# Keeping the FFN's hidden values in PSUM pairs through the FP4 quantizer, in a planned kernel

## The chip, the cores and the metric

The kernel runs on one core of a Trainium2 chip. A core has a matrix engine (PE, whose weight loads are shown apart as PEld), a vector engine (DVE), a scalar engine (ACT), GpSimd (POOL), a queue that issues transfers (SP) and sixteen DMA engines. On-chip memory is SBUF, and PSUM with eight banks of 512 float32 values in each of 128 partitions; PE writes its products to PSUM. The metric is the device time of one execution in microseconds, the median of several runs.

## The reference

The input x has shape (4, 2048, 256). Four residual layers follow each other, each on the layer-normed x: attention A, an FFN, attention B, and the same FFN once more.

```python
def fp4_quant_dequant(x):          # blocks of 16 along the last dim
    xb = x.reshape(shape[:-1] + (shape[-1] // BLOCK, BLOCK))
    scale = jnp.max(jnp.abs(xb), axis=-1, keepdims=True) / 6.0
    scale = jnp.maximum(scale, jnp.float32(1e-12))
    xn = xb / scale
    idx = jnp.searchsorted(_MID, jnp.abs(xn))
    q = _GRID[idx] * jnp.sign(xn) * scale
...
    gate = fp4_linear(x, w_gate)   # 256 -> 704
    y = fp4_linear(x, w_up)        # 256 -> 704
    h = jax.nn.silu(gate) * y
    return fp4_linear(h, w_down)   # 704 -> 256
...
    x = x + _L0_attn_a_ref(_layernorm(x), ...)
    x = x + _L0_ffn_ref(_layernorm(x), ...)
    x = x + _L0_attn_b_ref(_layernorm(x), ...)
    x = x + _L0_ffn_ref(_layernorm(x), ...)
```

`fp4_linear` quantizes both its input and its weight. Attention B mixes the four samples that share a position (its first axis); attention A needs two norms over the whole tensor, which a first pass over x supplies.

## The kernel before

**Tiles.** There are 16 groups j of 128 positions, each with four samples s, so a group is a tile of [128, 4, 256]. In each group the two FFNs (k = 1 and 2) handle one sample at a time: 16 x 2 x 4 = 128 FFN tiles of [128 rows, 704 hidden values].

**The plan.** Nothing is issued in the order of the source. `plan.op(engine, us, rank, fn, reads, writes, ...)` records an operation with its engine, a cost in microseconds and a due time; tokens of the form (buffer, part) give the dependences. `Plan.order` then lists the operations by a simple simulation of the engines: of the operations that are ready on an engine, the one due first is taken, provided that its buffers are free. A buffer is taken from its pool by the first operation that names it and goes back after the last one. `LATE` and `SYNC` are delays between an operation and one that depends on it on another engine; on the same engine the delay is 0. An operation with `port=True` keeps such operations of DVE and POOL apart in the plan. `BEGIN` holds six offsets for each group, the due times of its stages. Each engine then executes its list in order and waits at semaphores.

**PSUM.** Eight banks in two pools of four: `mm` for the hidden products and the first pass's weight products, `bank` for all else (transposes, projections, the down product).

**An FFN tile** (`ffn_tile`, L1436) goes through these steps:

1. PE, L1447: for each half of 352 columns, the gate product into one `mm` bank and the up product into another; two chunks of 128 along the contraction, and two records in the trace for each float32 matmul.
2. ACT, L1468: silu of the gate bank into the SBUF tile `sil`.
3. DVE, L1479: `sil` times the up bank into the SBUF tile `h` (pool of 3). `h` has 17 columns for each block of 16; the seventeenth holds 6e-12, the floor of the block's largest value.
4. `to_grid` (L1209): DVE takes each block's largest absolute value with the padding column (L387) and its reciprocal (L388), both in one planned operation; DVE multiplies `h` by -6 times the reciprocal into `qa` (L392); ACT writes |qa| x 2^22 as bfloat16 into `qm` (L398), whose rounding is the grid's; DVE takes max(qm, floor) + qa in place (L405) and max(qm, floor) - qa into `qm` (L408). These three DVE passes are marked `port=True`.
5. `scales_turned` (L1278): PE transposes the tile's 44 scales (L1286), ACT copies them (L1294), SP spreads them over `hqT` by six transfers (L1303).
6. SP transposes `qm` into `gT` by a DMA (L1505); POOL multiplies `hqT` by `gT` (L1514).
7. PE makes the down product from `hqT` (L1551); DVE adds it to x (L339, or L1583 in the second FFN, after which SP stores x, L1591).

The last group's second FFN multiplies the scales in before the transpose and transposes on PE (L1527), with `qa` kept.

**Around it.** The FFN's input is quantized likewise in tiles of 1024 (`xn`, `qax`, `qmx`). `turn` (L1146) transposes a group with PE and ACT; `project` (L1175) makes attention's products; L1329 drains a 512-wide product with a per-row factor; L1784 adds halves of attention B's weighted values in SBUF; L718 floors the scales of the weights; L1053 and L1080 belong to the weights' preparation, which runs once.

Of the kernel before, what the change touches and what calls it, by code (L numbers as in the profile page):

```python
# [12 lines left out]
BF16 = mybir.dt.bfloat16  # L13
# [5 lines left out]
P = 128  # L19
D = 256  # L20
# [4 lines left out]
HF = FF // 2  # L25
FB = FF // BLK

# [30 lines left out]
class Plan:  # L58
# [4 lines left out]
    SYNC = {"POOL": 0.12}  # L63
    LATE = {"PE": 0.163, "DVE": 0.08, "ACT": 0.097, "POOL": 0.04}
# [50 lines left out]
    def order(self, seed):  # L115
# [58 lines left out]
        while left:  # L174
# [58 lines left out]
            while done and done[0][0] <= now + 1e-9:  # L233
# [8 lines left out]
                for n in ops[i]["then"]:  # L242
                    ops[n]["left"] -= 1
                    f = ops[n]["engine"]
                    late = 0.0 if f == e else self.LATE.get(e, 0.0) + self.SYNC.get(f, 0.035)
# [8 lines left out]
def kernel(  # L254
# [43 lines left out]
    banks = [one([P, 512], f"bank{i}", ps) for i in range(8)]  # L298
# [86 lines left out]
    def to_scales(src, amax, rs):  # L385

        nc.vector.tensor_reduce(amax, src, AX.X, ALU.max, apply_absolute_value=True)  # L387
        nc.vector.reciprocal(rs, amax)  # L388

# [30 lines left out]
    plan.pool("mm", banks[:4])  # L420
    plan.pool("bank", banks[4:])
# [4 lines left out]
    floored += tiles("h", 3, [P, FB, BLK + 1], fp)  # L426
# [3 lines left out]
    tiles("sil", 2, [P, HF], fp)  # L430
    tiles("qa", 3, [P, FF], fp)

    for t in tiles("qm", 2, [P, 6 * P], fp, BF16):
        nc.gpsimd.memset(t[:, FF:], 0.0)
    tiles("gT", 2, [P, 6, P], fp, BF16)
# [3 lines left out]
    for t in tiles("hqT", 3, [P, 6, P], fp):  # L439
        nc.gpsimd.memset(t[P // 2 :, 5, :], 0.0)  # L440
# [15 lines left out]
    def first_pass():  # L456
        op = plan.op
        GRAM = [plan.given("bank", 2) for _ in range(KC)]
        gram = [b.ap for b in GRAM]

# [194 lines left out]
        for ns in together:  # L655
# [39 lines left out]
            if n >= SOON:  # L695
                op("POOL", 4.635, at + 3.0, lambda cut=cut: roots_later(cut), seen, done)
            else:
                y, _, v = (norm_tiles["a"][:, cut, i, :] for i in range(2, 5))
                op("DVE", 0.592, at + 0.5, lambda cut=cut: variances(cut), seen, done)
                op(  # L700
                    "ACT",
                    0.194,
# [6 lines left out]
                op("DVE", 0.962, at - 30.0, lambda cut=cut: inverses(cut), (), done)  # L709
# [119 lines left out]
        for i in range(2):  # L829
# [7 lines left out]
            for h in range(2):  # L837
# [10 lines left out]
                op("PE", 0.328, at + 8, turn, [(a, 0)], [(tp, 0)])  # L848
# [24 lines left out]
            0.622,  # L873
# [14 lines left out]
            0.407,  # L888
# [6 lines left out]
        def fold(at, dst, token, lhs):  # L895

            mm = plan.buf("mm")

            def pe():
# [19 lines left out]
                0.372,  # L919
# [6 lines left out]
        def center(at, w, n, tokens, bias=None):  # L926
# [3 lines left out]
            mm = plan.buf("mm")  # L930
# [48 lines left out]
        def times_biases():  # L979
# [15 lines left out]
            2.828,  # L995
# [14 lines left out]
        def take_sums():  # L1010
# [3 lines left out]

        op("DVE", 0.28, FIRST, take_g00, [(b, 0) for b in GRAM], [(G, 0)])
        op("DVE", 0.474, FIRST, take_rest, [(b, 0) for b in GRAM], [(G, 1)])
        op(
            "DVE", 0.847, FIRST + 1.0, take_sums, [(b, 0) for b in GRAM] + [("cross", 0)], [("part", 1)]
        )
        for c in range(KC):  # L1020
            mm = plan.buf("mm")
# [10 lines left out]
            def square(c=c, mm=mm):  # L1032
# [13 lines left out]
                "DVE", 0.714, FIRST, square, [(mm, 0), (WQK, 0)], [(PROD, c), ("part", 2 + c)]  # L1046
            )

        tot = plan.buf("mm")

        def total():
# [9 lines left out]
            0.187,  # L1061
# [8 lines left out]
            0.172,  # L1070
# [16 lines left out]
        def join_biases():  # L1087
# [7 lines left out]
        op("DVE", 2.447, FIRST, join_weights, [(MK, "m")], [("rn", 0), ("wvz z", 0)])  # L1095
        op(
            "DVE",
            1.501,
# [12 lines left out]
        (-456, -237, -412, -522, 134, -290),  # L1111
        (-168, -284, -45, 104, -606, 332),
        (119, 225, 211, 262, 362, 408),
        (143, 422, 246, 352, 80, 421),
        (147, 285, 233, 408, -700, 482),
        (388, -717, 369, 471, 380, 544),
        (460, -155, 484, 464, 544, 653),
        (536, -344, 284, 622, 569, 721),
        (545, 595, 595, 701, 520, 834),
        (563, 82, 635, -690, 342, 187),  # L1120
        (626, 675, 709, 812, 126, 892),
        (600, 340, 689, 490, 597, 906),
        (647, 956, 776, 896, 236, 1043),
        (705, 1053, 316, 796, 610, 936),
        (889, -178, 774, 528, -698, 1416),
        (873, 1096, 427, 1046, 274, 496),
    ]

    def group(j):

        begin = BEGIN[j][0]
        X = kept[j] if j in kept else plan.buf("x")
# [753 lines left out]
```

## Time and profile before

| | |
|---|---|
| Time, median of 3 runs | 1492.98 us (1492.23 to 1496.39) |
| The profiled execution | 1495.64 us |
| Its span, first to last instruction | 1493.9 us |
| Instructions in the span | 19989 |
| Mean granted PE clock | 0.999 |
| DMA | 220990 packets, 96.87 MB |
| HBM | 18.09 MB read, 8.39 MB written |
| First hidden product | 114.6 us after the span's start |
| Last hidden product ends | some 1472.1 us |

The page gives busy time for each engine and then in 40 slices of the span, where a digit is a tenth of busy time. Groups of instructions are shown with their line, engine, operation, output and input tiles, shapes and count; behind the bar come the idle time before them and what ended it. "Mean" durations include the part of an instruction that overlaps the next one's start. The views by source line add the least, the median and the largest duration. Some lines of the 40 slices:

```profile
PE   7989999999999999999999999999999999999998
DVE  6899999999899899999999999999898999999985
ACT  6556646543745463666565465453357443555332
POOL 5344656625746354653635555662747354565442
```

and of the engines' idle time, by what was waited for (total us, times, longest):

```profile
POOL hqT L1514 <- DMA gT<-qm: 128.0, 33, 11.1
ACT qm L398 <- DVE qa L392: 109.5, 64, 5.3
ACT qm L398 <- DMA gT<-qm: 26.4, 11, 5.4
PE bank L1551 <- POOL hqT L1514: 10.9, 14, 1.9
PE bank L1447 <- DVE h L1479: 4.9, 5, 1.8
```

### The profile page before, as it was taken

Reading aid. Unit: us, or ns where it says so; the run is one execution under the profiler, and the core shown is the slowest. Engines: PE = TensorE matmul, PEld = TensorE weight load, DVE = VectorE, ACT = ScalarE, POOL = GpSimd, SP = SyncE. Lnnn points to the kernel's source line nnn. Section 1 sums busy time; section 2 is a strip of 40 time slices with the busy share of each in tenths; the row PEclk is TensorE's granted clock in tenths of the full one; section 3 lists DMA queues with packets and bytes.
Section 4 is the critical chain, followed back from the end, with each engine's and each line's share of the span. In section 5 each row is a group of like instructions: output and inputs, shape, how many; then the busy total and the mean of one; then the engine's idle time right before and its main releaser. Section 6 shows DMA issues by size and latency. Waiting matters only on the chain.

```text
span 1493.9 us, 19989 instructions
## 1 busy us (share of the span) xinstructions
PE 1440.6 (96%) x5742; PEld 998.6 (67%) x5742; DVE 1373.4 (92%) x2139; ACT 793.4 (53%) x1694; POOL 767.5 (51%) x787
## 2 busy tenths in 40 slices
PE   7989999999999999999999999999999999999998
PEld 6746666667666666766666666666766656767776
DVE  6899999999899899999999999999898999999985
ACT  6556646543745463666565465453357443555332
POOL 5344656625746354653635555662747354565442
PEclk9999999999999999999999999999999999999999
DMA  8403321234432324434223322332522423423441
GB/s 255 119 0 49 53 53 28 40 61 88 70 60 54 67 54 86 84 74 62 34 48 56 68 54 50 67 55 50 103 39 41 75 48 67 66 40 72 85 85 35
DMA packets 220990, 96.87 MB, mean 65 GB/s; under 512 B 108240, under 2 KB 220624, under 8 KB 220880
## 3 DMA queue, kind: packets, MB, share of 16 engines
q1 hardware_dynamic: 220880, 95.60, 32.9%
q8 instruction: 45, 0.74, 0.2%
q14 instruction: 65, 0.53, 0.1%
HBM read 18.09 MB, written 8.39 MB: 18 GB/s over the span
## 4 chain that ended last, share of the span: by engine, by line
PE 58%; DVE 25%; issue 5%; DMA 4%; ACT 4%; POOL 4%; SPq 0%; POOLq 0%; ACTq 0%; DVEq 0%
PE bank L1447 27%; PE bank L1551 14%; PE bank L1177 12%; DVE qa L405 3%; PE bank L1154 2%; DVE qa L392 2%; DVE pp L1658 2%; DVE qm L408 2%; DVE h L1479 2%; DVE sh L387 2%; DVE sc L1665 2%; DMA gT<-qm 2%; DVE x L339 1%; POOL hqT L1514 1%; DVE vz L1329 1%
## 5 line engine op out<-in xcount | busy, mean ns | idle before, releaser
L1447 PE MATMUL bank<-wguT,turned 128*128 128x352 f32 x2048 | 637.0, 461 | 7.7 <-DVE h L1479 4.9
L1447 PEld LDWEIGHTS bank<-wguT,turned 128*128 128x128 f32 x2048 | 380.5, 190 | 213.4 <-issue 12.5
L1514 POOL TENSOR_TENSOR hqT<-hqT,gT 128x768 f32<-128x768 f32 x124 | 229.2, 1852 | 304.2 <-DMA gT<-qm 128.0
L1551 PE MATMUL bank<-wdT,hqT 128*128 128x256 f32 x1536 | 352.5, 381 | 11.6 <-POOL hqT L1514 10.9
L1551 PEld LDWEIGHTS bank<-wdT,hqT 128*128 128x128 f32 x1536 | 288.7, 190 | 73.7 <-POOL hqT L1514 21.5
L398 ACT ACTIVATE qm<-qa 128x704 bf16<-128x704 f32 (+2 forms) x136 | 105.9, 780 | 142.1 <-DVE qa L392 109.5
L1468 ACT ACTIVATE sil<-bank 128x352 f32<-128x352 f32 x256 | 114.7, 455 | 110.3 <-PE bank L1447 88.0
L405 DVE SCALAR_TENSOR_TENSOR qa<-qm,qa 128x704 f32<-128x704 bf16 (+2 forms) x136 | 147.9, 1088 | 15.1 <-ACT qm L398 14.8
L1479 DVE TENSOR_TENSOR h<-sil,bank 128x352 f32<-128x352 f32 x256 | 128.6, 509 | 29.3 <-ACT sil L1468 17.3
L1766 POOL TENSOR_TENSOR pp<-vg,sc 128x1024 f32<-128x1024 f32 x64 | 137.8, 2169 | 23.9 <-DVE tok L1787 20.9
L392 DVE SCALAR_TENSOR_TENSOR qa<-sh,h 128x704 f32<-128x704 f32 x128 | 132.2, 1040 | 1.1
L408 DVE SCALAR_TENSOR_TENSOR qm<-qm,qa 128x704 bf16<-128x704 bf16 x124 | 126.9, 1024 | 2.5
L1177 PE MATMUL bank<-wvz,turned 128*128 128x512 f32 x256 | 117.5, 596 | 8.1 <-ACT turned L1161 4.5
L387 DVE TENSOR_REDUCE sh<-h 128x44 f32<-128x748 f32 x128 | 119.1, 931 | 3.8
L1177 PE MATMUL bank<-wqkB,turned 128*128 128x512 f32 x256 | 120.5, 593 | 0.9 <-ACT qk L1646 0.9
L1270 POOL TENSOR_TENSOR qax<-qax,sx 128x1024 f32<-128x1024 f32 x32 | 70.1, 2190 | 75.1 <-DVE qax L408 65.0
L1161 ACT COPY turned<-bank 128x512 f32<-128x512 f32 x160 | 85.9, 586 | 30.5 <-PE bank L1154 30.3
L345 ACT ACTIVATE dev<-x,norms_f 128x256 f32<-128x256 f32 x128 | 64.8, 506 | 46.3 <-DVE x L339 43.8
L1177 PEld LDWEIGHTS bank<-wvz,turned 128*128 128x128 f32 x256 | 46.6, 190 | 57.4 <-issue 40.6
L1658 DVE TENSOR_TENSOR pp<-qk 128x1024 f32<-128x1024 f32 x64 | 82.0, 1281 | 1.9 <-ACT qk L1646 1.9
L381 ACT ACTIVATE xn<-x,norms_f 128x256 f32<-128x256 f32 x128 | 67.6, 591 | 21.8 <-POOL norms_f L375 16.5
L1665 DVE TENSOR_REDUCE sc<-pp 128x64 f32<-128x1024 f32 x64 | 77.8, 1215 | 1.3
(193 smaller groups left out, 2030.2 us busy)
## 6 DMA issues: line engine op xcount, KB each, us to landing
hqT<-sT SPq DMA_DIRECT2D x620, 64.0 KB
x<-in_L_attn_a_x_dram SPq DMA_DIRECT2D x23, 512.0 KB
out_dram<-x SPq DMA_DIRECT2D x64, 128.0 KB
hqT<-sT SPq DMA_DIRECT2D x124, 32.0 KB
gT<-qm SPq DMA_TRANSPOSE x124
hqT<-in_L_ffn_w_down_dram SPq DMA_DIRECT2D x2, 352.0 KB
hqT<-in_L_ffn_w_gate_dram SPq DMA_DIRECT2D x5, 128.0 KB
hqT<-in_L_ffn_w_up_dram SPq DMA_DIRECT2D x5, 128.0 KB
```

The costliest lines, as they stand in the source:

```text
L387: nc.vector.tensor_reduce(amax, src, AX.X, ALU.max, apply_absolute_value=True)
L392: nc.vector.scalar_tensor_tensor(blocks(a), over_blocks(rs), -6.0 * BELOW, src, ALU.mult, ALU.mult)
L405: nc.vector.scalar_tensor_tensor(a, m, FLOOR, a, ALU.max, ALU.add)
L408: nc.vector.scalar_tensor_tensor(a if to is None else to, m, FLOOR, a, ALU.max, ALU.subtract)
L1177: nc.tensor.matmul(bank.ap[:, :n], lhs.ap[:, c, s * P : (s + 1) * P], w[:, c, :], start=(c == 0), stop=(c == KC - 1),)
L1447: nc.tensor.matmul(bank.ap[:, :HF], xqT.ap[:, c, s * P : (s + 1) * P], w[:, c, cols], start=(c == 0), stop=(c == KC - 1),)
L1468: lambda g=g, sil=sil: nc.scalar.activation(sil.ap, g.ap[:, :HF], AF.Silu),
L1479: lambda u=u, sil=sil, half=half: nc.vector.tensor_mul(h.ap[:, half * FB // 2 : (half + 1) * FB // 2, :BLK], blocks(sil.ap), blocks(u.ap[: ...
L1514: lambda: nc.gpsimd.tensor_mul(hqT.ap, hqT.ap, gT.ap),
L1551: nc.tensor.matmul(o.ap[:, :D], hqT.ap[:, i, :], wdT[:, i, :], start=(i == 0), stop=(i == 5),)
L1658: nc.vector.tensor_mul(pr.ap, qk.ap[:, s : s + 1, :D].to_broadcast([P, S, D]), qk.ap[:, :, D:],)
L1766: nc.gpsimd.tensor_mul(pv.ap.rearrange("p t (n e) -> p t n e", e=HD), vg.ap[:, :, :D].rearrange("p t (n e) -> p t n e", e=HD), over_blocks ...
```

## The change

**PSUM and pools.** The eight banks become two pairs of two banks and four single banks; the pool `mm` and the tile `h` are gone. The gate product of the first 512 columns takes a single bank; a pair takes the up product (704 values over both banks), the gate product of the last 192 columns behind it, and, once those are used, the 44 block maxima. `qa` goes from 3 tiles to 2, `qm` from 2 to 4, `gT` from 2 to 3 and `hqT` from 3 to 4. `sil` becomes two kinds of tile, of 512 and 192.

**The FFN tile.** The hidden product is cut at 512 instead of 352. DVE multiplies `sil` into the up values in place, in PSUM. The reduction reads PSUM without a padding column and writes the maxima to PSUM; a new DVE operation applies the floor into `sh`; the reciprocal is an operation by itself. The passes run in place in PSUM and the last one writes `qm` (or `qa`) in SBUF. They are no longer marked `port=True`.

**The plan.** `SAME` adds a delay between dependent operations of one engine; many costs are smaller by about as much, and others are set anew. Further tokens ("place") make an operation claim a later buffer of its chain early: the first gate product claims the pair, the spread of scales claims `qm` or finds it claimed, the transposing DMA claims `hqT`, the projections claim `vz`, `qk` and `vg`. `BEGIN` holds new numbers throughout. The input quantizer's maximum and reciprocal also become two operations.

```diff
-HF = FF // 2
+HA = 512
+GE = FF + FF - HA
...
+    SAME = {"DVE": 0.125, "ACT": 0.13, "POOL": 0.12}
...
-                    late = 0.0 if f == e else self.LATE.get(e, 0.0) + self.SYNC.get(f, 0.035)
+                    late = self.SAME.get(e, 0.0)
+                    if f != e:
+                        late = self.LATE.get(e, 0.0) + self.SYNC.get(f, 0.035)
...
-    banks = [one([P, 512], f"bank{i}", ps) for i in range(8)]
+    pairs = [one([P, 2, 512], f"pair{i}", ps) for i in range(2)]
+    banks = [one([P, 512], f"bank{i}", ps) for i in range(4)]
...
-    plan.pool("mm", banks[:4])
-    plan.pool("bank", banks[4:])
+    plan.pool("pair", pairs)
+    plan.pool("bank", banks)
...
-    for t in tiles("qm", 2, [P, 6 * P], fp, BF16):
+    for t in tiles("qm", 4, [P, 6 * P], fp, BF16):
...
+            g, u, qm, sh = (plan.buf(p) for p in ("bank", "pair", "qm", "sh"))
+            sil = [plan.buf("sil"), plan.buf("silB")]
+            qa = None if apart else plan.buf("qa")
+
+            def flat(n0=0, n1=FF):
+                return u.ap.rearrange("p t n -> p (t n)")[:, n0:n1]
...
+            def rest():
+                product(flat(HA, FF), wuT, HA, FF)
+                product(flat(FF, GE), wgT, HA, FF)
...
+            op(
+                "PE", 1.717, at, lambda: product(g.ap[:, :HA], wgT, 0, HA), x_w, [(g, 0), (u, "place")]
+            )
+            op(
+                "PE", 1.717, at + 1.7, lambda: product(flat(0, HA), wuT, 0, HA), x_w, [(u, 0)]
+            )
+            op("PE", 1.295, at + 3.4, rest, x_w, [(u, 1), (u, "gate")])
...
+                    lambda half=half, n0=n0, n1=n1: nc.vector.tensor_mul(
+                        flat(n0, n1), sil[half].ap, flat(n0, n1)
                     ),
-                    [(u, 0), (sil, 0)],
-                    [(h, half)],
+                    [(u, 0), (u, 1), (sil[half], 0)],
+                    [(u, half)] + ([(u, "gate")] if half else []),
...
+            def hidden_largest():
+                nc.vector.tensor_reduce(
+                    flat(GE, GE + FB), blocks(flat()), AX.X, ALU.max, apply_absolute_value=True
+                )
+
+            def hidden_floor():
+                nc.vector.tensor_scalar(
+                    sh.ap[:, 0, :], flat(GE, GE + FB), 6e-12, 0.0, ALU.max, ALU.add
+                )
+
+            def hidden_over_scales():
+                over_scales(flat(), blocks(flat()), sh.ap[:, 2, :])
+
+            def hidden_steps():
+                to_steps(qm.ap[:, :FF], flat())
+
+            def hidden_sum():
+                to_sum(flat(), qm.ap[:, :FF])
+
+            def hidden_grid():
+                from_sum(flat(), qm.ap[:, :FF], qm.ap[:, :FF] if apart else qa.ap)
...
+            op("DVE", 0.8, at + 6, hidden_largest, HU, [(u, "amax")])
+            op("DVE", 0.1, at + 6.5, hidden_floor, [(u, "amax")], [(sh, 0)])
...
-            op("SP", 4.9, at + 1, spread, [(sT, 0)], [(dst, "scale")], land=2.7)
+            op("SP", 4.9, at + 1, spread, [(sT, 0)], [(dst, "scale"), (with_it, "place")], land=2.7)
...
-                    [(gT, 0)],
-                    land=1.75,
+                    [(gT, 0), (hqT, "place")],
+                    land=1.9,
```

## The prediction

> **What bounds the kernel now.** First the page's busy times and the shares of the chain that ended last:
>
> ```profile
> PE 1440.6 (96%) x5742; PEld 998.6 (67%) x5742; DVE 1373.4 (92%) x2139; ACT 793.4 (53%) x1694; POOL 767.5 (51%) x787
> ...
> PE 58%; DVE 25%; issue 5%; DMA 4%; ACT 4%; POOL 4%; SPq 0%; POOLq 0%; ACTq 0%; DVEq 0%
> ```
>
> Two engines are nearly full. PE is the first bound, DVE the second, and the chain passes from one to the other. Then the busy time by stage:
>
> ```profile
> 100.00:1400.00 1300.00, 1265.72 (x4954) 868.68 (x4953) 1222.85 (x1818) 704.94 (x1498) 686.69 (x636) 1.00 0.32 59
> 0.00:100.00 100.00, 86.62 (x423) 65.16 (x424) 79.41 (x212) 58.10 (x124) 44.18 (x124) 1.00 0.46 140
> 1400.00:1494.00 94.00, 88.27 (x368) 64.77 (x366) 71.14 (x111) 30.40 (x72) 36.64 (x27) 1.00 0.31 64
> ```
>
> The columns are the stretch, its length, then PE, PEld, DVE, ACT and POOL busy, clock, DMA share, GB/s. In the middle PE idles 34 us of 1300 and DVE 77 us; the clock is full throughout. Third, the DVE instructions of the FFN tile, by line (min/median/max ns) and by form (mean ns last before the bar):
>
> ```profile
> L408 DVE SCALAR_TENSOR_TENSOR qm<-qm,qa x124: 827/891/2621, 124.7 to 1454.6; 128x704 bf16<-128x704 bf16 x124
> L1479 DVE TENSOR_TENSOR h<-sil,bank x256: 461/514/525, 119.6 to 1474.0; 128x352 f32<-128x352 f32 x128
> L387 DVE TENSOR_REDUCE sh<-h x128: 917/932/933, 120.5 to 1474.5; 128x44 f32<-128x748 f32 x128
> ```
> ```profile
> L405 DVE SCALAR_TENSOR_TENSOR qa<-qm,qa 128x704 f32<-128x704 bf16 x130 | 144.1, 1108 | 15.1 <-ACT qm L398 14.8
> L392 DVE SCALAR_TENSOR_TENSOR qa<-sh,h 128x704 f32<-128x704 f32 x128 | 132.2, 1040 | 1.1
> L408 DVE SCALAR_TENSOR_TENSOR qm<-qm,qa 128x704 bf16<-128x704 bf16 x124 | 126.9, 1024 | 2.5
> L1329 DVE SCALAR_TENSOR_TENSOR vz<-bank,norms_a,bvz 128x512 f32<-128x512 f32 x64 | 45.4, 727 | 1.2 <-PE bank L1177 1.0
> L1784 DVE TENSOR_TENSOR pp<-pp 128x512 f32<-128x512 f32 x64 | 55.2, 862 | 0.0
> ```
>
> The passes L392, L405 and L408 take two SBUF tensors; their medians are 886, 884 and 891 ns but their tails reach 2.6 us. L1479, with one tensor in PSUM, never exceeds 525 ns, and the one-tensor reduce L387 never 933. The timeline says what stretches the passes:
>
> ```profile
> 820.33 2.25 POOL L1514 TENSOR_TENSOR hqT<-hqT,gT 128x768 f32<-128x768 f32 x1
> ...
> 821.33 2.00 DVE L408 SCALAR_TENSOR_TENSOR qm<-qm,qa 128x704 bf16<-128x704 bf16 x1
> ```
>
> L408 begins inside POOL's multiply, which ends at 822.58, and finishes 0.75 us later: it stood until POOL was done. POOL pays too: L1514 has a median of 1647 ns and a mean of 1852.
>
> **The change part by part.** I price DVE work first as engine time, then as path time. By line the chain holds 2.5% of L405, 2.2% of L392 and 2.0% of L408, so 37, 33 and 30 us of 1493.9. For DVE work in general I use DVE's chain share over its busy time: 0.25 x 1493.9 / 1373.4 = 27%.
>
> *Passes leave SBUF.* After the change each pass reads one SBUF tensor (scales or qm) and one PSUM tensor, the kind that never stretched. Excess of mean over median: L405 224 ns x 130, L392 154 x 128, L408 133 x 124 = 29.1 + 19.7 + 16.5 = 65 us of DVE. On the chain: 37 x 224/1108 + 33 x 154/1040 + 30 x 133/1024 = 7.5 + 4.9 + 3.9 = **-16.3 us**. For POOL, (1852 - 1647) x 124 = 25 us, 11% of its time; L1514 holds 1% of the chain (15 us): **-1.7**.
>
> *Reduce and floor.* The reduce reads 704 instead of 748 elements: 44 x 1.05 ns (the slope between L1583, 414 ns for 256, and L1784, 684 for 512) is 46 ns of 931 on 1.9% of the chain (28 us): **-1.4**. The padding column gives way to a separate DVE instruction on 44 elements. Nearest row: the 32- and 44-element TENSOR_SCALAR L718, median 184 ns, of which about 80 overlap the next instruction, so 0.10 x 128 = 13 us of DVE, 27% of it **+3.6**. A dependent DVE instruction starts 30 ns after its source's end instead of 80 before it, 0.11 us lost. In the built order such neighbours (reduce-reciprocal, reciprocal-pass, sum-grid) were 128 + 37 + 80 = 245; with the floor they are 59 + 70 + 72 + 48 = 249. The planner's new same-engine delays thus pay for the extra link only: 0.
>
> *PE, ACT, DMA.* A tile's 16 records of 352 columns become 8 of 512 and 8 of 192. The chain shows 32 of 352 in 9.47 us (296 ns each) and 8 of 512 in 3.44 (430); 192 follows at 162. 16 x 296 = 4.74 us, 8 x 430 + 8 x 162 = 4.74: 0. A weight load is recorded at 190 ns, longer than 162; were that the pace it would cost 28 ns x 8 x 128 = 29 us of PE. But ten loads of L1053, before 2-column matmuls, start within 1.0 us, 111 ns apart, so I take 0. ACT: two silu of 455 ns become about 589 and 324; the Abs pass reads PSUM, about 40 ns less; ACT is 53% busy, so 0 (were it the bound, still a gain). The six spreads and the transpose per tile stay; only their places on SP's queue move, with one more gT and hqT and two more qm, which removes ACT's 26 us wait for gT<-qm, off the path: 0, or 0.25 of it, 6 us, if ACT were on it. First multiply: it waits for the whole hidden product, about 2.4 us later; DVE's other instructions cover that (mean 4.1 us of foreign DVE work between a tile's first multiply and its grid pass in the new order); uncovered it would be charged in the slot rival below.
>
> *PSUM writes by DVE.* Two multiplies, the reduce and two passes per tile write PSUM; no row shows DVE doing that. Reading it costs nothing: L1583 takes 414 ns for 256 with a bank, L339 417 with a bank and 419 without. Nearest dear row: L1329's median of 744 against L1784's 684, +60 ns. Bounds: 0 to 60 x 5 x 128 = 38 us, 27% of it 10. I take 0, since +60 goes with L1329's per-partition scalar: L1080 has one without PSUM and takes 484 for 256. That a bank could not be read and written at once is not excluded by a DVE row; PE's accumulating matmuls, at the 459 ns of the first ones, speak against it.
>
> The Trainium skill speaks against this part (Perfetto Trace Analysis, Optimizing Scalar/DVE Operations): DVE's fixed access overhead is given as about 60 ns on SBUF and 125 on PSUM. The rows above do not show it for reads; by it, 4 moved instructions x 65 ns x 128 = 33 us, and the sum would be some 9 us worse.
>
> *Ends.* After the last hidden product the old kernel runs 21.8 us (1472.1 to 1493.9) with 17 us of PE work; the new order leaves 11.5 us of PE work behind it. The last tile's own steps, by the rows, need about 17 to 19: **-3**, between 0 and -5.
>
> *New order.* Buffers claimed early and new due times move nearly every instruction. PE's work at its shown intervals: 606 (L1447) + 332 (L1551) + 220 (512-wide) + 63 + 55 (288, 256) + 84 (transposes) + 65 (first pass, rest) = 1425. Adding 7.5 before the first matmul, 3.3 after the last and 6 in the first pass gives 1442, the floor. So order can bring at most about 28 beyond the above; at worst the slot rival's loss. DVE work between a tile's first multiply and its grid pass falls from 16.8 to 8.6 us, so tiles go through faster, but PE depends on it more closely. I take **-6**.
>
> Sum: -16.3 - 1.7 - 1.4 + 3.6 - 3 - 6 = -24.8; the profiled span becomes 1469. The profiled execution took 1495.64 with its surroundings, 2.7 above the median of runs (1492.98); the median becomes **1468**.
>
> **Rivals.** *PE's stalls close (0.14).* With DVE at some 1315 us of 1448 (91%) PE never waits: 1443 to 1455, say 1448. For: 34 us of idle PE have many small releasers (POOL, DVE, ACT). Against: only two pairs.
>
> *Nothing (0.10).* PE is 96% busy and DVE's relief falls off the path; POOL and ends against the floor instruction: 1493 - 1.7 - 3 + 3.6 = 1492.
>
> *Slot loop, slower (0.18).* Before, banks came free at the multiply, and three h tiles followed; now a pair is held from the up product to the grid pass, and only two exist. PE stands before the product that claims a pair; behind it on PE wait down products, projections and scale transposes, and on them DVE's adds and POOL. A pair is held for about 3.0 (products) + 0.6 (silu) + 8.6 = 12.2 us on average, in the worst ten tiles 16 to 26; PE's work between two uses of a pair is 20.4 on average but 12.1 to 16.0 in 30 of 126. An average stall of 0.35 us a tile costs 45: 1468 + 45 = 1513. From 0.19 us a tile (24.8/128) it decides.
>
> *Dear PSUM writes, slower (0.12).* If each of 640 writes costs 150 ns more, 96 us of DVE, 26 on the path, 1494; from there on slower. At half rate, 2.2 us a tile, DVE needs 1373 - 65 - 6 + 13 + 280 = 1595 and with its 120 us of idling 1715.
>
> **Numbers.** The forecast, 1457 to 1486, has 0.46. Faster by over 0.3% (4.5 us, about what a measurement of this kernel can tell from no change): 0.46 + 0.14 = 0.60; within it 0.10; slower 0.18 + 0.12 = 0.30. The range 1443 to 1512 reaches from the PE floor to the slot loop's price and holds all but the worse half of the slower cases.
>
> **What would show it.** Passes in PSUM at 0.88 us median with no tail over 1 us; DVE busy near 1315; L1514's counterpart near 1.7 us mean; hidden products 4.74 us a tile; the tail after the last hidden product under 20 us. Wrong: medians above 1.0 us (dear writes), or PE idle before the hidden products released by the grid pass (slot loop).

## The result, and the profile after

The changed kernel takes **1501.42 us** (median of 6 runs, 1500.36 to 1503.18); beside it on the same chip the kernel before took 1495.5. The ratio is 1.0045, with a 95% interval of 1.003 to 1.006: slower by half a per cent, where 1468 and faster was forecast. The profiled execution took 1503.18 us, its span 1501.4, against 1493.9 before. PE's granted clock is 0.997, so the clock doesn't explain it.

From the page: the engines' busy time and the shares of the chain that ended last.

```profile
PE 1444.4 (96%) x5742; PEld 971.7 (65%) x5742; DVE 1303.7 (87%) x2267; ACT 797.2 (53%) x1694; POOL 671.3 (45%) x787
...
PE 53%; DVE 28%; ACT 6%; DMA 5%; POOL 4%; issue 3%; SPq 0%; POOLq 0%; ACTq 0%
```

DVE has lost 70 us of work and POOL 96, and the kernel is longer all the same. In the chain the share of PE has fallen (58% to 53%), and the shares of DVE (25% to 28%), ACT and DMA have risen: more of the time is spent in work that PE waits for. DVE's instructions of the FFN tile by form (busy us, mean ns of one, then idle before them), and POOL's product:

```profile
L405 DVE SCALAR_TENSOR_TENSOR pair<-qm,pair 128x704 f32<-128x704 bf16 x128 | 113.8, 890 | 43.7 <-ACT qm L398 43.4
L392 DVE SCALAR_TENSOR_TENSOR pair<-sh,pair 128x704 f32<-128x704 f32 x128 | 113.8, 889 | 2.3
L1504 DVE TENSOR_REDUCE pair<-pair 128x44 f32<-128x704 f32 x128 | 113.6, 890 | 1.8
L408 DVE SCALAR_TENSOR_TENSOR qm<-qm,pair 128x704 bf16<-128x704 bf16 x124 | 108.9, 879 | 1.3
```
```profile
L1563 POOL TENSOR_TENSOR hqT<-hqT,gT 128x768 f32<-128x768 f32 x124 | 211.8, 1710 | 449.8 <-DMA gT<-qm 236.6 <-DMA hqT<-sT 140.4 <-PE bank L1457 14.6
```

The means of the passes have come down from 1108, 1040 and 1024 ns to 890, 889 and 879, onto the old medians; the longest of them takes 897 ns, where it was 2.6 us. POOL's product fell from 1852 to 1710 ns. But it now stands idle 236.6 us for the transposing DMA, where that was 128.0. The stages (PE, PEld, DVE, ACT and POOL busy, clock, DMA share, GB/s):

```profile
0.00:100.00 100.00, 83.14 (x416) 63.62 (x417) 73.94 (x207) 55.86 (x119) 41.84 (x122) 0.98 0.48 140
100.00:1400.00 1300.00, 1265.77 (x4927) 839.47 (x4926) 1155.24 (x1934) 709.33 (x1500) 602.35 (x643) 1.00 0.34 58
```

In the middle DVE does 68 us less than before in the same 1300, and PE not a microsecond more. Where PE waits is in the engines' idle time by what was waited for (total us, times, longest), after and then before:

```profile
PE bank L1600 <- POOL hqT L1563: 13.2, 19, 1.8
...
PE bank L1296 <- DVE sh L1509: 8.1, 14, 2.2
```
```profile
PE bank L1286 <- DVE sh L387: 3.1, 4, 0.9
```

L1296 transposes the scales and L1600 is the down product. The waits for POOL rose from 10.9 to 13.2 us, those for the scales from 3.1 to 8.1, and these now name the floor, L1509. Both are ends of the same chain: largest value, floor, scales on one side; passes, transposing DMA, POOL's product on the other.

The waits view has fewer of these than the starts of PE's matmuls show (13.2 us before the down product, where the starts give 23.5), so I also added up stalls from the starts of PE's matmuls: the interval from each to the next, less the tenth percentile for its form, where that is over 25 ns, put down to the later one. Without stalls PE would need 1413.7 us in the kernel before and 1414.8 in the changed one: PE's own work is the same. The stalls are 64.7 and 71.6 us.

| kernel | time, us | stalls | before the down product | before the scale transposes | before the hidden products |
|---|---|---|---|---|---|
| before | 1495.5 | 64.7 | 17.6 | 5.4 | 11.8 |
| changed | 1501.4 | 71.6 | 23.5 | 13.2 | 3.4 |
| e2, before with one-input passes | 1475.1 | 44.5 | 5.9 | 3.7 | 5.6 |
| e3, changed without the floor | 1494.9 | 62.0 | 23.7 | 6.4 | 2.0 |
| e4, changed, POOL without gT | 1494.9 | 62.8 | 9.3 | 18.3 | 3.8 |
| e5, both | 1483.7 | 55.1 | 8.5 | 10.4 | 3.5 |
| kernel before in a new list | 1519.6 | 91.2 | 20.9 | 7.4 | 10.5 |
| changed data path, floor in the reduction, new list | 1489.5 | 58.1 | 12.6 | 5.9 | 4.5 |

### The profile page after: what moved, and what is told of

Read it like the earlier page. It is cut to its first block, busy times and chain, and to the rows that moved or that the text cites. A ratio compares the mean times of both kernels' runs of the same rounds, so it can differ in the third digit from the quotient of the medians.

```text
span 1501.4 us, 19855 instructions
## 1 busy us (share of the span) xinstructions
PE 1444.4 (96%) x5742; PEld 971.7 (65%) x5742; DVE 1303.7 (87%) x2267; ACT 797.2 (53%) x1694; POOL 671.3 (45%) x787
## 4 chain that ended last, share of the span: by engine, by line
PE 53%; DVE 28%; ACT 6%; DMA 5%; POOL 4%; issue 3%; SPq 0%; POOLq 0%; ACTq 0%
PE pair L1457 14%; PE bank L1177 13%; PE bank L1600 13%; PE bank L1457 7%; DMA gT<-qm 3%; DVE pair L1494 3%; DVE pair L1504 3%; PE bank L1154 2%; PE pair L581 2%; POOL hqT L1563 2%; DVE pp L1707 2%; DVE qm L408 2%; DVE sc L1714 2%; DVE pair L392 2%; DVE pair L405 1%
## 5 line engine op out<-in xcount | busy, mean ns | idle before, releaser
L1457 PE MATMUL pair<-wguT,turned 128*128 128x192 f32 (+1 forms) x1536 | 415.8, 416 | 0.1
L1563 POOL TENSOR_TENSOR hqT<-hqT,gT 128x768 f32<-128x768 f32 x124 | 211.8, 1710 | 449.8 <-DMA gT<-qm 236.6
L1600 PE MATMUL bank<-wdT,hqT 128*128 128x256 f32 x1536 | 354.3, 381 | 15.3 <-POOL hqT L1563 13.2
L1457 PEld LDWEIGHTS pair<-wguT,turned 128*128 128x128 f32 x1536 | 265.8, 190 | 145.2 <-issue 135.8
L1600 PEld LDWEIGHTS bank<-wdT,hqT 128*128 128x128 f32 x1536 | 287.2, 190 | 85.8 <-POOL hqT L1563 32.1
L1457 PE MATMUL bank<-wguT,turned 128*128 128x512 f32 x512 | 240.6, 593 | 0.4 <-DVE x L344 0.3
L405 DVE SCALAR_TENSOR_TENSOR pair<-qm,pair 128x704 f32<-128x704 bf16 x128 | 113.8, 890 | 43.7 <-ACT qm L398 43.4
L1457 PEld LDWEIGHTS bank<-wguT,turned 128*128 128x128 f32 x512 | 93.8, 190 | 79.3 <-issue 71.5
L398 ACT ACTIVATE qm<-pair 128x704 bf16<-128x704 f32 x128 | 96.6, 754 | 88.4 <-DVE pair L392 86.1
L1494 DVE TENSOR_TENSOR pair<-sil,pair 128x512 f32<-128x512 f32 x128 | 88.1, 689 | 39.6 <-ACT silB L1483 32.8
L392 DVE SCALAR_TENSOR_TENSOR pair<-sh,pair 128x704 f32<-128x704 f32 x128 | 113.8, 889 | 2.3
L1504 DVE TENSOR_REDUCE pair<-pair 128x44 f32<-128x704 f32 x128 | 113.6, 890 | 1.8
L408 DVE SCALAR_TENSOR_TENSOR qm<-qm,pair 128x704 bf16<-128x704 bf16 x124 | 108.9, 879 | 1.3
## 6 DMA issues: line engine op xcount, KB each, us to landing
out_dram<-x SPq DMA_DIRECT2D x64, 128.0 KB
hqT<-in_L_ffn_w_gate_dram SPq DMA_DIRECT2D x5, 128.0 KB
hqT<-in_L_ffn_w_up_dram SPq DMA_DIRECT2D x5, 128.0 KB
```

What stands on the lines that cost most here:

```text
L392: nc.vector.scalar_tensor_tensor(blocks(a), over_blocks(rs), -6.0 * BELOW, src, ALU.mult, ALU.mult)
L405: nc.vector.scalar_tensor_tensor(a, m, FLOOR, a, ALU.max, ALU.add)
L408: nc.vector.scalar_tensor_tensor(a if to is None else to, m, FLOOR, a, ALU.max, ALU.subtract)
L1457: nc.tensor.matmul(to, xqT.ap[:, c, s * P : (s + 1) * P], w[:, c, n0:n1], start=(c == 0), stop=(c == KC - 1),)
L1494: lambda half=half, n0=n0, n1=n1: nc.vector.tensor_mul(flat(n0, n1), sil[half].ap, flat(n0, n1)),
L1504: nc.vector.tensor_reduce(flat(GE, GE + FB), blocks(flat()), AX.X, ALU.max, apply_absolute_value=True)
```

## The experiments

"In its own order" means that the planner's list of operations was kept; only what an operation issues was changed. Each ratio, with its 95% interval, is to the kernel before on the same chip; it is estimated from all runs and can differ a little from the quotient of the medians. The intervals are some 2 us to either side, so a difference between two kernels is known to 2 to 4 us.

**Is the relief real?** Two runs take it from either side. The first gives the changed kernel its contention back:

```diff
-over_scales(flat(), blocks(flat()), sh.ap[:, 2, :])
+over_scales(flat(), blocks(wguT[:, 0, :FF]), sh.ap[:, 2, :])
...
```

> The changed kernel, order of every engine kept; the three quantizer passes of an FFN tile read their second tensor from an SBUF weight tile instead of the PSUM pair (the quantized values are then meaningless), so they can collide with GpSimd again. Theory A (PE alone sets the end, DVE's relief fell into DVE's idle time): the passes' means rise from 0.89 to about 1.05 us, DVE gets some 60 us busier, the time changes by less than 5 us from the changed kernel's 1501. Theory B (the relief is worth the 16 us on the path that the prediction gave it, and another part of the change costs over 20): 1515 to 1525.

Measured 1624.71 us, 1.0859 [1.0841, 1.0878]. Two of the three passes, by form:

```profile
L1520 DVE SCALAR_TENSOR_TENSOR pair<-qm,wguT 128x704 f32<-128x704 bf16 x128 | 167.5, 1309 | 42.8 <-ACT qm L398 42.5
L392 DVE SCALAR_TENSOR_TENSOR pair<-sh,wguT 128x704 f32<-128x704 f32 x128 | 164.6, 1287 | 2.3
```

The same instructions on the same number of elements take 1309 and 1287 ns with a second input in SBUF. The price, 123 us, is far outside both expectations. PE's stalls are 199.8 us. Why it is so much dearer than the relief in the other direction is not shown; that a list made without contention meets it unprepared is a guess. The second run takes the contention out of the kernel before, for all three passes; `one_input` is a tensor_reduce over the same 704 elements, which writes 44.

```diff
-over_scales(a.ap, v(), q.ap[:, 2, :])
+one_input(a.ap[:, :FB], v())
...
```

> The kernel before, order of every engine kept; the three passes of an FFN tile become one-input reductions over the same 704 elements (about 0.89 us each, nothing is quantized), so nothing of them can collide with GpSimd. Theory A: within 5 us of the kernel before. Theory B: 14 to 20 us faster than the kernel before, at about 1478.

Measured 1475.06 us, 0.9857 [0.984, 0.9874]. The three substitutes by form, PE's two waits, and the middle stage (columns as above):

```profile
L397 DVE TENSOR_REDUCE qa<-qm 128x44 f32<-128x704 bf16 x128 | 111.9, 874 | 14.3 <-ACT qm L401 14.0
L397 DVE TENSOR_REDUCE qa<-h 128x44 f32<-128x704 f32 x128 | 109.6, 863 | 0.0
L397 DVE TENSOR_REDUCE qm<-qa 128x44 bf16<-128x704 f32 x124 | 109.1, 880 | 2.5
```
```profile
PE bank L1557 <- POOL hqT L1520: 3.0, 6, 0.7
...
PE bank L1292 <- DVE sh L387: 2.2, 3, 1.0
```
```profile
100.00:1400.00 1300.00, 1280.95 (x5035) 883.15 (x5034) 1178.96 (x1846) 713.10 (x1511) 620.15 (x643) 1.00 0.33 60
```

The substitutes take about what the passes in PSUM take: 2617 ns for the three against 2658, which is 5 us of DVE in all tiles. Here the relief does reach PE: in the same 1300 us it is busy 1280.95 and not 1265.72, and waits 3.0 us for POOL and 2.2 for the scales. The relief is worth **21 us** in the list of the kernel before; the forecast had 18 (16.3 + 1.7). So the gain exists, less perhaps a microsecond or two for the shorter substitutes, and the change as a whole gives back some 26.

**What the floor costs, and POOL's wait.** The first of these two runs lets the reduction write the scale tile and issues no floor.

```diff
-    flat(GE, GE + FB), blocks(flat()), AX.X, ALU.max, ...
+    sh.ap[:, 0, :], blocks(flat()), AX.X, ALU.max, ...
...
-    nc.vector.tensor_scalar(sh.ap[:, 0, :], flat(GE, GE + FB), 6e-12, ...)
+    pass
...
```

> The changed kernel, order kept, without the floor instruction: the reduction writes the block maxima into the SBUF tile itself and the floor on them is left out. The scale transposes on PE, which waited 13 us for the floor's output (5 us for the reduction's before), get their input some 0.23 us earlier. If the floor's length on the tile's chain is what the change lost: 4 to 8 us faster than the changed kernel. If the order is (theory A): 0 to 4 us faster.

Measured 1494.93 us, 0.9997 [0.9986, 1.0008]: 6.5 us less than the changed kernel. The stalls before the scale transposes halve, from 13.2 to 6.4 us, and those before the down product stay. The next run lets POOL's product read `hqT` twice, so that it doesn't wait for the transposing DMA.

```diff
-nc.gpsimd.tensor_mul(hqT.ap, hqT.ap, gT.ap)
+nc.gpsimd.tensor_mul(hqT.ap, hqT.ap, hqT.ap)
```

> The changed kernel, order kept; GpSimd's product of a tile takes hqT twice and no longer reads the transposed gT (the values are not scaled grid values), so it does not wait for the transposing DMA, only for the spread of scales. GpSimd's start after the DMA's issue was 0.3 to 0.5 us later than the plan had it, and down products waited 17.5 us in all for GpSimd. If the DMA's lateness makes these waits (theory C): 6 to 12 us faster than the changed kernel; if it is hidden by the spread or by PE's other waits: within 4 us.

Measured 1494.9 us, 0.9992 [0.9981, 1.0003], again 6.5 less, inside what the expectation gave to the DMA. POOL's product in this run, by form:

```profile
L1563 POOL TENSOR_TENSOR hqT<-hqT 128x768 f32<-128x768 f32 x124 | 194.1, 1567 | 401.5 <-DMA hqT<-sT 340.9 <-PE bank L1177 17.0 <-PE bank L1296 11.0
```

The idle time before it is now put down to the spread of the scales. But the product is also shorter, 1567 ns against 1710 in the mean (medians 1467 and 1644), so the run doesn't tell the DMA's lateness from 0.14 us less of POOL in each tile; it shows what a shorter way to the down product is worth. The stalls before the down product fall by 14 us and those before the scale transposes rise by 5: with less at the one wait, PE loses more at the other. Both changes together:

> The changed kernel in its own order, without the floor instruction (the maximum goes straight to the scale tile) and with POOL's product reading hqT twice instead of gT, so both changes of the two last runs together; the floor and the transposed values are left out of the result. Each alone gave 6.5 us. Theory A (late links: the scale transposes behind the floor and the down projection behind POOL are what the new order lost, and relieving one only moves the wait to the other): clearly more than the sum, 1474 to 1484 us, PE waiting under 8 us for either. Theory B (two pairs hold the chain back, whatever comes after it): at most the sum, 1487 to 1494 us, with PE's waits ahead of the hidden products up from 3.4 us to 10 or more.

Measured 1483.71 us, 0.9925 [0.9913, 0.9937]: 17.7 us less, more than the 13 of the two alone. PE's two waits, by what was waited for:

```profile
PE bank L1296 <- DVE sh L1504: 7.2, 10, 1.6
...
PE bank L1598 <- POOL hqT L1561: 2.3, 5, 1.0
```

The wait for POOL went from 13.2 to 2.3 us, that for the scales only to 7.2. The time agrees with theory A (1474 to 1484), and its own condition of under 8 us for either wait is met in this view, though by the stalls the scales still have 10.4. Before the hidden products, where theory B wanted 10 us or more, 3.5 remain. So the two links, POOL's shorter product included, hold 17.7 of the 26 us that the change gave back; why the new order waits for them is the next question.

**Moving the floor.** First aside, so that the transposes need the reduction alone and only the reciprocal needs the floor:

```diff
-    flat(GE, GE + FB), blocks(flat()), AX.X, ALU.max, ...
+    sh.ap[:, 0, :], blocks(flat()), AX.X, ALU.max, ...
...
-    sh.ap[:, 0, :], flat(GE, GE + FB), 6e-12, 0.0, ALU.max, ALU.add
+    sh.ap[:, 2, :], sh.ap[:, 0, :], 6e-12, 0.0, ALU.max, ALU.add
...
-    nc.vector.reciprocal(sh.ap[:, 2, :], sh.ap[:, 0, :])
+    nc.vector.reciprocal(sh.ap[:, 2, :], sh.ap[:, 2, :])
```

> The changed kernel in its own order with the floor kept, but off the path of the scale transposes: the reduction writes the maximum to the scale tile in SBUF, the floor instruction makes its floored copy for the reciprocal alone. If the floor costs by what waits behind it on PE: about the 6.5 us of the run without it, 1494 to 1497 us. If it costs by DVE's time (128 x 195 ns, 25 us, and a row more of DVE's queue): under 2 us gained, 1499 to 1502 us.

Measured 1540.53 us, 1.0298 [1.0282, 1.0315], outside both expectations: 39 us more than the changed kernel. The source view of the floor (min/median/max ns), first here and then in the changed kernel, and its row by form here (busy us, mean ns):

```profile
L1509 DVE TENSOR_SCALAR sh<-sh x128: 116/186/2347, 125.0 to 1520.7; 128x44 f32<-128x44 f32 x128
```
```profile
L1509 DVE TENSOR_SCALAR sh<-pair x128: 131/196/204, 127.2 to 1487.2; 128x44 f32<-128x44 f32 x128
```
```profile
L1509 DVE TENSOR_SCALAR sh<-sh 128x44 f32<-128x44 f32 x128 | 64.8, 507 | 1.9
```

The same 44 elements read from SBUF and not from PSUM have a mean of 507 ns against 195. The timeline has the longest of them (start, us):

```profile
367.46 2.95 POOL L1663 TENSOR_TENSOR x<-x,boB 128x1024 f32<-128x1024 f32 x1 [1.38 <-ACT xh L386]
...
368.11 2.35 DVE L1509 TENSOR_SCALAR sh<-sh 128x44 f32<-128x44 f32 x1
```

It starts inside a POOL instruction and ends 0.05 us after that instruction's end (370.46 and 370.41). Of 128 floors 45 were longer than 250 ns; each of them started while a POOL instruction ran and ended 39 to 43 ns after that one's end. So this instruction with *one* SBUF input stands behind POOL like the two-input passes; the forecast had counted only those. The rows above agree with the Trainium skill (VectorE: DVE Perf Modes, What auto-detection actually checks), by which the engine takes a faster mode over both of its ports where a single source and the destination are in SBUF and their shapes allow it, and (GPSIMD Engine Reference, Key points) such a mode contends with GpSimd, as two SBUF inputs do. The faster mode itself can't be read from these rows, only the waiting. Reading the floor's input from PSUM, as the change does, avoids it: there 51 of 128 floors started with over 204 ns of a POOL instruction still to run, and none took more than 204.

The next run was meant to tell the floor's time from its latency. It keeps a PSUM source and moves the instruction behind the third pass; as in e3, the reduction writes the scale tile.

```diff
...
     from_sum(flat(), qm.ap[:, :FF], ...)
+    nc.vector.tensor_scalar(sh.ap[:, 1, :], flat(GE - FB, GE), 6e-12, ...)
...
```

> The changed kernel in its own order; the floor instruction has the same form and length (44 elements from PSUM, some 0.2 us), but stands behind the third pass, where neither the scale transposes nor the reciprocal wait for it; its result is unused and the scales have no floor. Theory latency (the floor costs because the transposes and the passes of its own tile stand behind it): 1494 to 1497 us, as without it. Theory time (25 us more of a DVE that sets the pace cost 6.5 us wherever they stand): 1500 to 1503 us.

Measured 1498.01 us, 1.001 [0.9999, 1.0021]. The moved instruction by form, and PE's waits for the scales:

```profile
L1522 DVE TENSOR_SCALAR sh<-pair 128x44 f32<-128x44 f32 x128 | 24.9, 195 | 0.0
```
```profile
PE bank L1296 <- DVE sh L1504: 3.3, 5, 1.8
```

The instruction is as long as in the changed kernel, the wait falls from 8.1 to 3.3 us. The time lies between the two expectations: the instruction costs 3.1 us here and 6.5 ahead of the transposes and the passes, each within 2 to 3 us. That isn't a clean split into time and latency. In the changed kernel the next DVE instruction starts 226 ns (median) after the floor's start, since it is mostly the reciprocal that needs the floor's output; here it starts after 114 ns, since nothing needs it. So some of the difference is DVE's time too. Then the same link in the list of the kernel before, on top of e2:

```diff
     nc.vector.tensor_reduce(amax, src, AX.X, ALU.max, ...)
+    nc.vector.tensor_reduce(amax, amax.unsqueeze(2), AX.X, ALU.max)
     nc.vector.reciprocal(rs, amax)
...
```

> The kernel before in its own order with its passes as one-input instructions (1475 us), and between the largest values and the reciprocal one more one-input instruction of 44 elements, as the floor of the change; the passes' values are not the quantizer's. The forecast's term, 3.6 us: 1477 to 1480 us. Theory list (the changed list, not the instruction, makes it dear): 1475 to 1478 us. Theory chain (any list pays what the chain gets longer): 1480 to 1484 us.

Measured 1480.49 us, 0.9895 [0.9876, 0.9915]: 5.4 us above e2, with an instruction of this length:

```profile
L389 DVE TENSOR_REDUCE sh<-sh x128: 198/199/201, 122.5 to 1460.5; 128x44 f32<-128x44 f32 x128
```

That is the lower end of theory chain, and 0.5 us above the range for the forecast's 3.6; at 2 to 4 us for a difference the two are not told apart. In either list the floor costs some 5 or 6 us. Relief and floor together would be 1480 to 1482 us; the changed kernel is 20 above that.

**A new list for the changed kernel.** Same instructions and buffers, other costs and starting ranks (`BEGIN`):

```diff
+    for o in plan.ops:
+        if o["engine"] in ("DVE", "ACT"):
+            o["us"] += 0.01
...
+        elif o["land"] in (1.75, 1.9, 2.7):
+            o["land"] += 0.45
     order = plan.order(0)
```

> The changed kernel with the same instructions and buffers, but another list: the planner is told 10 ns more for each DVE and ACT instruction, 40 ns more for POOL's products and 0.45 us more for the landing of the two DMAs of a tile, and its table of starting ranks was searched anew with these costs (some 300,000 lists). Theory A (the list in the change was tight against late links): faster than the changed kernel by 6 to 20 us, 1481 to 1495 us, with the down projection's and the scale transposes' waits down from 37 us together to under 25. Theory B (two pairs set the pace, no list helps): 1496 to 1510 us.

Measured 1503.25 us, 1.0053 [1.0039, 1.0068]: no gain, as theory B wanted. The longer search that also made the list of the faster version below (the run that the expectation speaks of) gave a third one:

> The instructions and buffers of the changed kernel untouched (its floor instruction too), with a list found by the same longer search as the run before it. Theory A: 1488 to 1498 us, below the changed kernel by 4 us or more. Theory B: 1499 to 1510 us, as the first replanned list gave 1503.3.

Measured 1510.8 us, 1.0099 [1.008, 1.0118]: theory A's forecast failed a second time, and the time is just above theory B's too. With the floor aside, read from SBUF as in e6:

> As the replanned kernel, with the floor aside as well (the scale transposes need the maximum alone) and a list searched anew for it with the same costs; its result is complete. Its planned end is 4.9 us before that of the replanned kernel. Theory A: 1474 to 1490 us, faster than both kernels. Theory B: 1492 to 1505 us.

Measured 1515.86 us, 1.0139 [1.0116, 1.0162]. That is above both expectations. Its floor has a mean of 482 ns, so it says nothing on the list.

By itself this looked like the pairs. But the trace doesn't show PE standing for a pair: from the end of a third pass to the start of the up product that writes the pair which it freed (counted two tiles on), the median is 3.6 us in the changed kernel, and only 2 of 126 are below 0.5. The gate product ahead of it, which claims the pair in the plan, comes nearer: its median is 1.4 us, and 28 of 126 are below 0.5. What lacked was the control, the kernel before in a list from the first of these searches.

> The kernel before, instructions and buffers untouched, but in a list searched anew with the later costs that were given to the replanned kernels. Theory list (a new list alone moves the time by as much as the rest of the change took, whatever the data path): off by 8 us or more, and rather slower, 1500 to 1515 us. Theory pairs (it is the two pairs that cost): 1488 to 1499 us, near the kernel before.

Measured 1519.56 us, 1.015 [1.0127, 1.0173]. Nothing but the list differs from the kernel before, and it costs **24 us**, more than either theory had. Its waits by what was waited for:

```profile
PE bank L1551 <- POOL hqT L1514: 7.5, 9, 1.9
PE bank L1551 <- issue: 6.1, 5, 3.0
PE bank L1154 <- ACT turned L1161: 5.5, 4, 3.2
PE bank L1447 <- DVE h L1479: 5.4, 4, 2.2
PE bank L1177 <- ACT turned L1161: 4.0, 7, 1.1
```

No wait stands out; they are many and small, 91.2 us of stalls against 64.7. So lists differ by as much as the whole question, and the list of the kernel before is better than this one. Whether the relief depends on it:

> The replanned kernel before (1519.6 us) with its three passes as one-input instructions that don't contend with POOL, as in the second run; the passes' values are not the quantizer's. If the relief is worth the same in any list and the lists make the rest: 1495 to 1502 us, and with the floor's 5 to 6.5 us on top the 1503.3 us of the replanned changed kernel. If the relief in the second run hung on the kernel before's own list: 1506 to 1520 us.

Measured 1495.1 us, 1.0002 [0.9993, 1.0012]: a relief of 24.5 us in this list, 20.7 in the other. With the floor (5.4 to 6.5) it comes to 1500.5 to 1501.6, beside the 1503.25 measured for the changed kernel in a new list made with the same costs. Between these lists the terms add up, and the change is worth 16 us of gain (1519.6 to 1503.3). That rests on one list of each; with the other new list of the changed kernel (1510.8) it is 9.

**A version that is faster.** The floor goes into the reduction: hidden blocks stand 17 elements apart in the pair, the products are cut at 480 and not at 512, and the seventeenth element holds the floor, written once per pair.

```diff
-HA = 512
+HA = 480
-GE = FF + FF - HA
+GE = 2 + (BLK + 1) * FB
...
+    def floor_column(pair):
+        flat = pair.rearrange("p t n -> p (t n)")[:, 2:GE]
+        nc.vector.memset(flat.rearrange("p (b k) -> p b k", k=BLK + 1)[:, :, BLK:], 6e-12)
...
-    flat(GE, GE + FB), blocks(flat()), AX.X, ALU.max, ...
+    sh.ap[:, 0, :], flat(k=BLK + 1), AX.X, ALU.max, ...
...
```

> The changed kernel in its own order, with the floor in the reduction instead of in an instruction: blocks of the hidden tile stand 17 elements apart in the PSUM pair (products of 480 and 224 columns instead of 512 and 192), the 17th holds the floor, written once per pair, and the reduction of 128 x 44 x 17 writes the scale tile directly. The result is complete. If the floor's 6.5 us come back and strided passes in PSUM cost nothing: 1493 to 1497 us, as in the run without a floor, passes at 0.88 to 0.90 us. If the stride in PSUM or the wider reduction costs what the floor did: 1498 to 1504 us, with longer means on the passes.

Measured 1500.78 us, 1.003 [1.0018, 1.0043]: 5.9 us above e3, though the passes keep their 0.88 to 0.89 us. The reduction has become 45 ns longer than e3's (928 against 883), and behind the last hidden product silu and multiply of 224 columns take 60 ns more than those of 192 (354 + 389 against 327 + 356). That is some 0.1 us more in each tile's chain. Whether it makes the 5.9 us, and which of the two, no run shows. In a searched list:

> The same data path (floor in the reduction, result complete), in another list: the planner gets 10 ns more for DVE and ACT, 40 ns more for POOL's products, 0.45 us more for the landing of a tile's two DMAs, and the table of starting ranks was searched for the least time with links still later than planned (DMA landings 0.6 to 0.9 us later). Theory A (the list of the change has no slack for late links, the two pairs don't bind): 1474 to 1488 us, PE's waits for POOL's product and for the scales together under 20 us against 37. Theory B (two pairs set the pace): 1493 us or more.

Measured **1489.53 us**, 0.9951 [0.9936, 0.9966], faster than the kernel before by 7 us and than the changed one by 12. Its waits and its middle stage:

```profile
PE bank L1609 <- POOL hqT L1572: 4.6, 10, 1.0
...
PE bank L1302 <- DVE sh L1515: 3.3, 6, 0.8
```

```profile
100.00:1400.00 1300.00, 1274.22 (x4987) 874.56 (x4987) 1164.88 (x1846) 722.43 (x1521) 628.07 (x654) 1.00 0.34 59
```

The two waits of the changed kernel, 13.2 and 8.1 us, are 4.6 and 3.3 here, and in the middle stage PE is busy 1274.22 us against 1265.77. The time itself is 1.5 us above theory A's range and below theory B's. A second list for it:

> The floor in the reduction, result complete, in a second list from an independent search with the same aim as the first (1489.5 us). Theory list: between 1478 and 1500 us, lists differ by about 10 us in what they leave of the gain; one of the two below 1490 us. Theory pairs: both at 1489 to 1492 us, since the pairs set it.

Measured 1495.38 us, 0.9994 [0.998, 1.0007]. With the same data path, three lists give 1489.5, 1495.4 and 1500.8.

## Why the prediction was wrong

The range, 1443 to 1512, holds the time, but by luck: it reaches so far through the slot rival's price, and the runs don't show that rival's wait. The direction is wrong. By its own steps:

- **"Passes leave SBUF", -16.3, and POOL, -1.7: right,** and somewhat small. Measured -20.7 in one list and -24.5 in another. All its signs came: passes at 0.88 us without a tail, DVE at 1303.7 us (1315 forecast), POOL's product at 1.71.
- **"Reduce and floor", -1.4 and +3.6: the floor was mis-sized.** It measured 6.5 us in the changed list and 5.4 in the old one. The step priced 0.10 us of DVE a tile, since it let 80 ns of the instruction overlap the next one. In the changed kernel the next DVE instruction starts 194 ns after the floor's start in the mean, because in 70 of 128 tiles it is the reciprocal, which must wait for the floor. So the floor takes 25 us of DVE and not 13; at the step's own share of 27% that is 6.8. The length was wrong, and the share fits at this place; behind the third pass the price was about half (e8). The reduce's own gain was not tried alone.
- **"PE, ACT, DMA", 0: right for PE,** 1414.8 against 1413.7 us without stalls. ACT's and the DMAs' parts were not measured by themselves; e4 takes out a wait for the transposing DMA, but shortens POOL's product as well.
- **"PSUM writes by DVE", 0: right.** The passes in place in PSUM take 889 and 890 ns. The Trainium skill's greater PSUM overhead (Perfetto Trace Analysis, Optimizing Scalar/DVE Operations) isn't seen in the durations of writes either.
- **"Ends", -3: nearly right for the end it names,** which became 16.7 us from 21.7, a gain of 5. But the first hidden product starts at 119.0 us and not at 114.6, which the step left out and which takes 4.4 of it back.
- **"New order", -6: the step that failed.** From the runs, 1475.1 for the relief, 5.4 for the floor, and 1501.4 in the end, the rest of the change, this step with the ends and the small terms, is worth about +20. It lies where PE waits for a tile's chain: against e2 PE's stalls are 27 us longer, the floor's part among them, with 17.6 more before the down product and 9.5 more before the scale transposes; shortening both links (e5) takes 17.7 us back. The step did say that PE would depend on DVE more closely, and still counted a gain. It asked what a list may gain (up to 28) and took its worst case from the slot rival. That a list can lose without any new limit was not weighed, though the diff replaces 94 of the 96 numbers of `BEGIN`. The kernel before loses 24 us when its list is replaced and nothing else.
- **The slower rivals** had the right sign and the wrong mechanisms. The slot loop would show as PE idle before the hidden products; stalls there fell from 11.8 to 3.4 us. Dear PSUM writes would show as longer passes.

**What stays open:** how much of the +20 is the two pairs, through the lists that they allow, and how much is this one list. For the data path with the floor as an instruction all three lists gave 1501 to 1511; with the floor in the reduction the best gave 1489.5, still 14 above e2. A list of two pairs that reaches 1480 was not found, and none was proven impossible. A third pair, which would leave two of the eight banks single, wasn't tried. One figure goes with the data path in every list: from the start of a tile's reduction to the start of its down product (the mean start of the one less that of the other) there are 31.4 us in the kernel before and 29.6 in its new list, but 20.3 in the changed kernel and 20 to 24 in the other lists with two pairs. So a late link has less time in which to hide. How much of the +20 this makes no run shows, and the kernel before loses 24 us in a list that keeps 29.6.

## What to carry to other kernels

When a change to a data path comes with a new plan, price the two apart: the old data path in a new list of the same effort is the control, and here it moved the time by 24 us, about as much as the relief was worth. Price a new link by where it stands and by what must wait for it: an instruction whose output the next one needs has no overlap to count on, and 0.2 us a tile cost 5 to 6.5 us in 128 tiles. And relief of an engine is collected only where the next engine stops waiting for it: see whether PE's busy share of a stage rises, not whether DVE's falls.

## What the hardware showed unexpectedly

- A DVE tensor_scalar on 44 elements with input and output in SBUF stood up to 2347 ns, until POOL was done (e6); from PSUM it never took more than 204. The same length as a reduction in SBUF (e9) took 198 to 201 ns, though 83 of 128 started inside a POOL instruction, and the reciprocal between SBUF tiles of that size never more than 430 (e6): of these three with one SBUF input only the tensor_scalar was held up.
- Reading and writing the same PSUM bank in one DVE instruction, with blocks 16 or 17 elements apart, costs nothing visible: passes of 704 elements take 876 to 890 ns in the mean either way, and 884 to 891 (median) between SBUF tiles before.
